# The range check's branch is moved from between the two layers to the end of the program, and layer 1's pools wait tile by tile

## The chip, the core and the metric

The kernel runs on one core of one Trainium2 chip. The metric is the device time of one execution in microseconds. Engines are named as in the profile: PE is TensorE's matmuls, PEld its weight loads, DVE is VectorE, ACT is ScalarE, POOL is GpSimd, SP is SyncE. A name with a q (SPq, PEldq, DVEq) is that engine's sequencer, which runs branches, waits, register loads and the issue of DMAs.

## What is computed

The input is x, float32 of shape (8, 256, 32, 32). Two layers follow each other:

```python
# layer 0, on images: attention and a gated convolutional block, each with a residual
a = attention(rms_norm(x))           # 1x1 conv -> 4 heads of softmax attention over 1024 positions, 3x3 depthwise conv
x = x + gamma1 * a
f = edffn(rms_norm(x))               # 1x1 conv -> 3x3 depthwise -> gelu(x1) * x2 -> 1x1 conv -> 8x8 FFT filter
x = x + gamma2 * f
# layer 1, on tokens t of shape (8, 1024, 256)
t = t + causal_attention(layer_norm(t))
t = t + mixture_of_8_experts(layer_norm(t))   # three 256x256 products each, gate from the mean over the batch
```

## The kernel before

The program is one straight line for each engine: all loops are unrolled when it is built. `pe`, `dve`, `act` and `pool` are wrappers (`InOrder`, recorded by the profile at L72) that keep their engine's instructions in the order in which the kernel calls them; what is called through `nc.` directly is placed by a scheduler. Loads and stores are issued by SP, in one queue.

**Layer 0.** The eight images are worked on in turn; attention of one image is woven with the convolutions of the one before. Softmax in layer 0 is taken without subtracting the maximum. That is exact as long as nothing overflows, so the sums and their reciprocals are kept in `accs`, and at the end of layer 0 they are compared with a limit. The last image's end runs alone: its last convolutions on DVE (`conv`, eight taps for each group), the products `pz`, `pf`, `py` on PE, and the additions into its tile `t` on DVE (from `py`). The image then goes to DRAM (`td`, L1114). A matrix `at`, needed by layer 1, is built from two weight matrices earlier in that stretch, in a tile `lin`, and also stored in DRAM (`at_d`, L1193).

**The branch.** `votes` (L1213, one matmul with one column) and `bad` (L1215, one element, on DVE) reduce the comparison to one integer. L1218 is

```python
with tc.If(nc.values_load(bad[0:1, 0:1]) > 0):
    layer0_shifted()
```

Each of the five engines loads `bad` into a register (TENSOR_LOAD), compares and branches (COMPARE_BRANCH). `layer0_shifted` is layer 0 again with the maximum subtracted. With the given inputs it is never run: all engines jump over it to a short block that brings the semaphores to the counts that the skipped part would have left and that waits for all DMAs of layer 0, the last store `td` among them.

**Layer 1.** Behind the branch the pool `wm` and the pools of layer 1 are opened. They stand on SBUF and PSUM that layer 0's pools had, and without `reuse_waits="tile"` their first instructions wait for what layer 0 left as a whole. SP issues, in this order, the vector `vec2` (L1231), `wrs`, `brs`, the first image `t` (L1376, 1 MB), `at` (L1380), `wv` (L1384), then two further images and the first expert weights `we` and `w`. `lower`, `mhalf1`, `sel` and `sel8` are constants that POOL builds.

The first image's layer norm is not woven with anything: PE transposes `t` into `tpt` (16 transposes), ACT copies to `zt`, DVE takes statistics (`st`, `mv`), POOL the power -1/2 (`y`, `r`), DVE scales `zt`, PE transposes back (`tpz`), ACT copies to `z`. Then PE forms keys (`pk`) and values (`pv`), and from there on the causal attention of one image is woven with the norms, keys and values of the next, and with `chores`, among them the splitting of the expert weights. At the head of DVE's share of layer 1 stand 19 small instructions that fold batch norm constants out of `vec2` (`bn_o` L175, `wrs`, `bn_s`, `s1a` to `s2b`, `bo`), and on ACT a table load and two square roots (L168).

**The expert stage.** Pools `hp`, `ps_a`, `ps_b`, `ps_q`, already with `reuse_waits="tile"`. PE is the bound; the last steps are an addition on DVE (`te`) and its store to `out` (L1808). The end of the program (L1986) is a block of waits for all semaphores and two barriers.

Of the kernel before, what the change touches and what calls it, by code (L numbers as in the profile page):

```python
# [104 lines left out]
def conv_attn_hybrid_kernel(  # L105
# [1111 lines left out]

    with tc.If(nc.values_load(bad[0:1, 0:1]) > 0):  # L1218
        layer0_shifted()

    z_d = [dram.tile([P, 2, 3, KC, HALF], F32, tag=f"zd{b}", name=f"zd{b}") for b in range(B)]
    u_d = [dram.tile([P, KC, N], F32, tag=f"ud{b}", name=f"ud{b}") for b in range(B)]
    wm = ctx.enter_context(tc.tile_pool(name="wm", bufs=1))
    more.append(wm.tile([P, NVEC - NVEC0], F32, name="vec2"))  # L1230
    nc.sync.dma_start(more[0], vecs[:, NVEC0:])  # L1231
    wrs = wm.tile([P, KC, NE], F32, name="wrs")
    nc.sync.dma_start(wrs, wr.rearrange("(k p) e -> p k e", p=P))
    brs = wm.tile([1, NE], F32, name="brs")
    nc.sync.dma_start(brs, br)
    wT = wm.tile([4 * NE, N], F32R, name="wT")
    feats = [wm.tile([P, KC, HALF], F32, name="feat0"), None]
    z2_last = wm.tile([P, KC, HALF], F32, name="z2_last")
    mhalf1 = wm.tile([P, NT], F32, name="mhalf1")
    nc.gpsimd.memset(mhalf1, -0.5)  # L1240

    NG, SLOTS = 2, NE // 2
    w_d = [[dram.tile([P, 3, KC, C], F32, tag=f"wd{e}_{l}", name=f"wd{e}_{l}") for l in range(3)] for e in range(NE)]
    w_in = {}

    def in_parts(e, l):

        return l != 1 or e % 2 == 1

    def load_expert(pool_, e, l):  # L1250

        tag = f"w{e % SLOTS}_{l}"
        if not in_parts(e, l):
            w_ = pool_.tile([P, KC, C], F32, tag=tag, name=tag, bufs=1)
            nc.sync.dma_start(w_, w2[e].rearrange("(k p) o -> p k o", p=P))
        else:
            w_ = pool_.tile([P, 3, KC, C], F32R, tag=tag, name=tag, bufs=1)
            nc.sync.dma_start(w_.bitcast(F32), w_d[e][l])
        w_in[e, l] = w_

    def stacked(dst, src, order):

        first = [order.index(i) for i in range(2)]
        dve.tensor_copy(dst[:, :, first[0]].bitcast(F32R), src)
        dve.tensor_sub(dst[:, :, first[1]].bitcast(F32R), src, dst[:, :, first[0]])
        for i, part in enumerate(order):
            if i not in first:
                dve.tensor_copy(dst[:, :, i], dst[:, :, first[part]])

    def upper(dst, src, eng=None, positive=False):  # L1270

        if eng is None:
            act.activation(dst[:, 0], src, AF.Relu if positive else AF.Copy, scale=DOWN)
        else:
            eng.tensor_scalar_mul(dst[:, 0], src, DOWN)

    def lower_part(dst, src, positive=False):
        high = dst[:, 0].bitcast(F32)
        if positive:
            dve.scalar_tensor_tensor(dst[:, 1], src, 0.0, high, ALU.max, ALU.subtract)  # L1280
        else:
            dve.tensor_sub(dst[:, 1], src, high)

    def difference(dst):
        dve.scalar_tensor_tensor(dst[:, 2], dst[:, 1].bitcast(F32), -STEP, dst[:, 0].bitcast(F32), ALU.mult, ALU.add)

    def layer_norm(src, dst, zt, room, bank):

        n = src.shape[2] // P
        mv = room([P, NT, 2], "mv", 2)  # L1290
        for i0 in range(0, n, 2):
            tp = bank([P, 2, C], "tpt")
            for i in range(2):
                for k in range(KC):
                    c0 = (i0 + i) * P
                    pe.transpose(tp[:, i, k * P : (k + 1) * P], src[:, k, c0 : c0 + P], ident)
            act.copy(zt[:, i0 : i0 + 2, :], tp)
            yield 0.6
            for i in range(i0, i0 + 2):
                st = room([P, 6], "st", 4)  # L1300
                dve.bn_stats(st, zt[:, i, :])
                dve.bn_aggr(mv[:, i, :], st)
            yield 0.6

        y = room([P, NT], "y1", 2)[:, :n]
        r = room([P, NT], "r1", 2)[:, :n]
        pool.tensor_scalar(y, mv[:, :n, 1], LN_EPS, None, ALU.add)
        pool.tensor_tensor(r, y, mhalf1[:, :n], ALU.pow)
        pool.tensor_mul(y, y, r)
        pool.tensor_mul(y, y, r)  # L1310
        pool.tensor_scalar(y, y, -0.5, 1.5, ALU.mult, ALU.add)
        pool.tensor_mul(r, r, y)

        for _ in range(4):
            yield 1.0

        def scaled(i0):
            for i in range(i0, i0 + 2):
                dve.tensor_scalar(zt[:, i, :], zt[:, i, :], mv[:, i, 0:1], r[:, i : i + 1], ALU.subtract, ALU.mult)

        scaled(0)
        yield 1.0
        scaled(2)
        yield 1.0
        for i0 in range(0, n, 2):
            if i0 + 4 < n:
                scaled(i0 + 4)
            tp = bank([P, KC, 2, P], "tpz")
            for i in range(2):
                for k in range(KC):  # L1330
                    pe.transpose(tp[:, k, i, :], zt[:, i0 + i, k * P : (k + 1) * P], ident)
            act.copy(dst[:, :, i0 * P : (i0 + 2) * P], tp.rearrange("p k i c -> p k (i c)"))
            yield 0.9

    def gate(h, room, bank):

        nt = NT // 2
        lg = bank([P, nt, NE], "lg")
        for i in range(nt):
            c0 = i * P  # L1340
            for k in range(KC):
                pe.matmul(lg[:, i, :], feats[h][:, k, c0 : c0 + P], wrs[:, k, :], start=(k == 0), stop=False)
            pe.matmul(lg[:, i, :], ones[0:1, :], brs, start=False, stop=True)
        yield 2.0
        ge = room([P, nt, NE], "ge", 1)
        gs = room([P, nt], "gs", 1)
        dve.tensor_reduce(gs, lg, AX.X, ALU.max)
        dve.tensor_sub(ge, lg, gs.unsqueeze(2).to_broadcast([P, nt, NE]))
        act.activation(ge, ge, AF.Exp)
        yield 1.0  # L1350
        dve.tensor_reduce(gs, ge, AX.X, ALU.add)
        dve.reciprocal(gs, gs)
        dve.tensor_mul(ge, ge, gs.unsqueeze(2).to_broadcast([P, nt, NE]))
        ge4 = room([P, nt, 4, NE], "ge4", 1)
        stacked(ge4, ge, (0, 1, 0, 1))
        yield 1.0
        pwT = bank([4 * NE, HALF], "pwT")
        for i in range(nt):
            pe.transpose(pwT[:, i * P : (i + 1) * P], ge4[:, i].rearrange("p a e -> p (a e)"), ident)
        dve.tensor_copy(wT[:, h * HALF : (h + 1) * HALF], pwT)  # L1360
        yield 0.5

    z = {}

    with ExitStack() as l1:
        wpool = l1.enter_context(tc.tile_pool(name="w1", bufs=1))
        one = l1.enter_context(tc.tile_pool(name="one1", bufs=1))
        two = l1.enter_context(tc.tile_pool(name="two1", bufs=2))
        tiny = l1.enter_context(tc.tile_pool(name="tiny1", bufs=4))
        ps_s = l1.enter_context(tc.tile_pool(name="ps_s1", bufs=2, space=PSUM))  # L1370
        ps_t = l1.enter_context(tc.tile_pool(name="ps_t1", bufs=2, space=PSUM))
        ps_m = l1.enter_context(tc.tile_pool(name="ps_m1", bufs=2, space=PSUM))

        def load_t(b):
            t[b] = two.tile([P, KC, N], F32, tag="t", name="t1", bufs=3)
            nc.sync.dma_start(t[b], t_d[b])  # L1376

        load_t(0)
        at = wpool.tile([P, KC, C], F32, name="at")
        nc.sync.dma_start(at, at_d)  # L1380

        def load_w(name, src):
            w_ = two.tile([P, KC, C], F32, tag=name, name=name, bufs=1)
            nc.sync.dma_start(w_, src.rearrange("(k p) o -> p k o", p=P))  # L1384
            return w_

        wv_s = load_w("wv", wvT)
        feats[1] = wpool.tile([P, KC, HALF], F32, name="feat1")
        load_t(1)


        lower = wpool.tile([P, P], F32, name="lower")
        nc.gpsimd.memset(lower, 1.0)
        nc.gpsimd.affine_select(
            out=lower, in_=lower, compare_op=ALU.is_ge, fill=0.0, base=0, pattern=[[-1, P]], channel_multiplier=1,
        )

        parts_w = two.tile([P, 3, KC, C], F32R, name="parts_w", bufs=1)
# [12 lines left out]
        def expert_parts():  # L1411

            for e in range(NE):
                for l, src in enumerate((w1, w2, wo)):
                    if not in_parts(e, l):
                        continue
# [75 lines left out]
        def until(what):  # L1492
            while what not in done:
                yield 0.7
# [152 lines left out]

# [336 lines left out]
```

## Time and profile before

| | us |
|---|---|
| median of 3 runs | 3183.1 (3177.89 to 3192.05) |
| the profiled execution: its own time | 3183.65 |
| its span, from the first to the last instruction | 3181.8 |
| PE busy | 2935.8 (92%) |
| DVE busy | 2390.2 (75%) |
| mean granted TensorE clock | 0.967 |

The profile is of one execution. Its time exceeds its span by 1.85 us. Times below are counted from the start of the span. A matmul's end is modelled, so busy time of PE says where PE has work, not how well it does it. A wait for several things is put down to the one that came last.

### The profile page before, as it was taken

What the parts mean: (1) busy time and instruction counts of PE and PEld (TensorE: products, weight loads), DVE (VectorE), ACT (ScalarE), POOL (GpSimd) and SP (SyncE); (2) the same over time, 40 slices, a digit from 0 to 9 for tenths busy, and PEclk for the clock granted to TensorE, in tenths of its full rate; (3) what the DMA queues carried; (4) which work ended last, traced back from release to release, by engine and by line L of the source; (5) the groups of instructions that cost most, each with busy time, mean ns of one, the idle gap of its engine ahead of it and who ended that gap; (6) DMA issues with size and microseconds to landing.
All of it is one profiled execution on the core that took longest, in us unless ns stands there. A gap on an engine that the chain in (4) does not pass through costs nothing.

```text
span 3181.8 us, 41598 instructions
## 1 busy us (share of the span) xinstructions
PE 2935.8 (92%) x16802; PEld 1938.8 (61%) x16802; DVE 2390.2 (75%) x3014; ACT 1565.1 (49%) x2312; POOL 341.0 (11%) x419
## 2 busy tenths in 40 slices
PE   5998899899898989868999999999999999999998
PEld 3654555555555555434666666677777777777776
DVE  1378877878787869664767665588988888888887
ACT  1554445555454536313333333365666666666665
POOL 1021211111111110001222222100000000000000
PEclk9998999999999999988999999999999999999999
DMA  5113030212112020002333221422112142211220
GB/s 152 55 27 80 27 80 27 72 36 62 46 47 61 28 66 8 17 14 101 125 131 132 106 103 54 176 76 78 69 67 82 64 172 86 99 67 66 93 73 27
DMA packets 63854, 234.85 MB, mean 74 GB/s; under 512 B 5590, under 2 KB 13862, under 8 KB 54822
## 3 DMA queue, kind: packets, MB, share of 16 engines
q1 hardware_dynamic: 63654, 232.12, 21.9%
q8 instruction: 134, 2.20, 0.3%
q14 instruction: 66, 0.54, 0.1%
HBM read 140.61 MB, written 91.49 MB: 73 GB/s over the span
## 4 chain that ended last, share of the span: by engine, by line
PE 49%; DVE 4%; ACT 1%; issue 0%; POOL 0%; SPq 0%; DMA 0%; ACTq 0%; DVEq 0%
PE pm L72 12%; PE pa L72 11%; PE q L72 11%; PE s L72 4%; PE po L72 4%; PE pv L72 2%; PE pk L72 2%; DVE zt L72 1%; DVE nm L72 1%; PE tp L72 1%; DVE pr L72 1%; PE tpz L72 1%; PE tpt L72 1%; DVE st L72 1%; ACT pr L72 1%
## 5 line engine op out<-in xcount | busy, mean ns | idle before, releaser
L72 PE MATMUL pa<-ze,w 128*128 128x512 f32 x1488 | 423.2, 393 | 0.0
L72 DVE SCALAR_TENSOR_TENSOR x<-hpad,vec,x 128x1024 f32<-128x1024 f32 x248 | 317.0, 1282 | 40.5 <-ACT x L72 33.5
L72 DVE SCALAR_TENSOR_TENSOR conv<-hpad,vec,conv 128x1024 f32<-128x1024 f32 x256 | 329.3, 1293 | 13.9 <-ACT conv L72 7.3
L72 PEld LDWEIGHTS pa<-ze,w 128*128 128x128 f32 x1488 | 278.2, 188 | 63.3 <-issue 3.1
L72 ACT ACTIVATE h<-pa,bn_o,s1a 128x512 f32<-128x512 f32 x256 | 198.7, 776 | 203.4 <-PE pa L72 203.4
L72 ACT ACTIVATE pT<-s 128x1024 f32<-128x1024 f32 x256 | 247.3, 1024 | 71.9 <-PE s L72 71.9
L72 PE MATMUL po<-pT,vT 128*32 128x256 f32 x4096 | 274.0, 385 | 0.0
L72 PE MATMUL q<-h2p,w 128*128 128x512 f32 x768 | 269.0, 459 | 0.0
L72 DVE SCALAR_TENSOR_TENSOR h<-pa,s1b,h 128x512 f32<-128x512 f32 x256 | 191.2, 747 | 93.9 <-PE pa L72 87.8
L72 PE MATMUL ph<-xn,piw 128*128 128x512 f32 x512 | 244.7, 615 | 3.1 <-DVE xn L72 1.6
L72 PE MATMUL pm<-h,w 128*128 128x512 f32 x512 | 240.8, 593 | 0.0
L72 PE MATMUL s<-kk,z 128*128 128x512 f32 x512 | 236.8, 594 | 4.1 <-DVE pr L72 4.1
L72 PE MATMUL q<-z_first,w 128*128 128x512 f32 x768 | 217.2, 391 | 2.7 <-DVE z_first L72 1.7
L72 PE MATMUL pm<-h1p,w 128*128 128x512 f32 x768 | 216.7, 390 | 0.5 <-DVE h1p L72 0.5
L72 DVE SCALAR_TENSOR_TENSOR o<-vpad,pe_w,o 128x1024 f32<-128x1024 f32 x128 | 163.5, 1282 | 45.5 <-ACT o L72 42.3
L72 PEld LDWEIGHTS q<-h2p,w 128*128 128x128 f32 x768 | 144.6, 188 | 83.1 <-issue 59.6
L72 PE MATMUL s<-qst,kst 128*128 128x256 f32 x1024 | 176.1, 314 | 14.5 <-DMA kst<-part 13.2
L72 ACT ACTIVATE hpad<-ph,pi_o 128x512 f32<-128x512 f32 x126 | 86.9, 689 | 182.9 <-PE ph L72 176.0
L72 PEld LDWEIGHTS po<-pT,vT 128*32 128x32 f32 x4096 | 120.8, 110 | 85.9 <-issue 4.2
L72 PEld LDWEIGHTS s<-qst,kst 128*128 128x128 f32 x1024 | 137.5, 193 | 47.8 <-issue 42.9
L72 PEld LDWEIGHTS q<-z_first,w 128*128 128x128 f32 x768 | 144.4, 188 | 34.4 <-DVE z_first L72 2.9
L72 PEld LDWEIGHTS pm<-h1p,w 128*128 128x128 f32 x768 | 144.7, 188 | 31.7 <-DVE h1p L72 0.9
(268 smaller groups left out, 5068.1 us busy)
## 6 DMA issues: line engine op xcount, KB each, us to landing
ze<-zd SPq DMA_DIRECT2D x29, 1536.0 KB, 6.4
qst<-part SPq DMA_DIRECT2D x32, 512.0 KB, 8.7
kst<-part SPq DMA_DIRECT2D x32, 512.0 KB, 14.9
te<-ud SPq DMA_DIRECT2D x32, 512.0 KB, 4.1
wd<-parts_w SPq DMA_DIRECT2D x20, 768.0 KB, 3.7
w<-wd SPq DMA_DIRECT2D x20, 768.0 KB, 4.6
zd<-parts SPq DMA_DIRECT2D x14, 1024.0 KB, 3.8
t<-in_x_dram SPq DMA_DIRECT2D x8, 1024.0 KB, 5.0
```

Of the source, the lines that this page charges most:

```text
L72: return self._tc.keep_in_program_order(method(*args, **kwargs))
```

## The change

Everything from the opening of `wm` to the end of the expert stage becomes a function `tokens(stack)`. It is called once without a condition, straight behind layer 0, and then a second time inside the branch, which now stands at the end of the program: if `bad` is set, layer 0 is run again with the maximum subtracted, and both later layers after it. `wm` and the seven pools of layer 1 get `reuse_waits="tile"`, so that a tile waits for the last users of the memory it stands on, and not for a whole pool. The first three loads of layer 1 (`t` of the first image, `at`, `wv`) are issued by POOL instead of SP, in POOL's program order. `wv` moves from one pool to another. What is left out (...) is the same code, indented once more.

```diff
-    with tc.If(nc.values_load(bad[0:1, 0:1]) > 0):
-        layer0_shifted()
+    NG, SLOTS = 2, NE // 2
     z_d = [dram.tile([P, 2, 3, KC, HALF], F32, tag=f"zd{b}", name=f"zd{b}") for b in range(B)]
     u_d = [dram.tile([P, KC, N], F32, tag=f"ud{b}", name=f"ud{b}") for b in range(B)]
-    wm = ctx.enter_context(tc.tile_pool(name="wm", bufs=1))
-    more.append(wm.tile([P, NVEC - NVEC0], F32, name="vec2"))
+    w_d = [[dram.tile([P, 3, KC, C], F32, tag=f"wd{e}_{l}", name=f"wd{e}_{l}") for l in range(3)] for e in range(NE)]
+
+    def tokens(stack):
+
+        wm = stack.enter_context(tc.tile_pool(name="wm", bufs=1, reuse_waits="tile"))
+        more[:] = [wm.tile([P, NVEC - NVEC0], F32, name="vec2")]
         nc.sync.dma_start(more[0], vecs[:, NVEC0:])
...
         with ExitStack() as l1:
-            wpool = l1.enter_context(tc.tile_pool(name="w1", bufs=1))
-            one = l1.enter_context(tc.tile_pool(name="one1", bufs=1))
-            two = l1.enter_context(tc.tile_pool(name="two1", bufs=2))
-            tiny = l1.enter_context(tc.tile_pool(name="tiny1", bufs=4))
-            ps_s = l1.enter_context(tc.tile_pool(name="ps_s1", bufs=2, space=PSUM))
-            ps_t = l1.enter_context(tc.tile_pool(name="ps_t1", bufs=2, space=PSUM))
-            ps_m = l1.enter_context(tc.tile_pool(name="ps_m1", bufs=2, space=PSUM))
+            wpool = l1.enter_context(tc.tile_pool(name="w1", bufs=1, reuse_waits="tile"))
+            one = l1.enter_context(tc.tile_pool(name="one1", bufs=1, reuse_waits="tile"))
+            two = l1.enter_context(tc.tile_pool(name="two1", bufs=2, reuse_waits="tile"))
+            tiny = l1.enter_context(tc.tile_pool(name="tiny1", bufs=4, reuse_waits="tile"))
+            ps_s = l1.enter_context(tc.tile_pool(name="ps_s1", bufs=2, space=PSUM, reuse_waits="tile"))
+            ps_t = l1.enter_context(tc.tile_pool(name="ps_t1", bufs=2, space=PSUM, reuse_waits="tile"))
+            ps_m = l1.enter_context(tc.tile_pool(name="ps_m1", bufs=2, space=PSUM, reuse_waits="tile"))
 
-            def load_t(b):
+            def load_t(b, queue=nc.sync):
                 t[b] = two.tile([P, KC, N], F32, tag="t", name="t1", bufs=3)
-                nc.sync.dma_start(t[b], t_d[b])
+                queue.dma_start(t[b], t_d[b])
 
-            load_t(0)
+            load_t(0, pool)
             at = wpool.tile([P, KC, C], F32, name="at")
-            nc.sync.dma_start(at, at_d)
-
-            def load_w(name, src):
-                w_ = two.tile([P, KC, C], F32, tag=name, name=name, bufs=1)
-                nc.sync.dma_start(w_, src.rearrange("(k p) o -> p k o", p=P))
-                return w_
-
-            wv_s = load_w("wv", wvT)
+            pool.dma_start(at, at_d)
+            wv_s = wpool.tile([P, KC, C], F32, name="wv")
+            pool.dma_start(wv_s, wvT.rearrange("(k p) o -> p k o", p=P))
             feats[1] = wpool.tile([P, KC, HALF], F32, name="feat1")
             load_t(1)
...
+    with ExitStack() as stack:
+        tokens(stack)
+
+    with tc.If(nc.values_load(bad[0:1, 0:1]) > 0):
+        layer0_shifted()
+        with ExitStack() as stack:
+            tokens(stack)
```

## The prediction

> **What bounds the kernel now.** I read the table of windows first, around the place of the branch and behind it. Its columns are the window, its length, busy time of each engine with its number of instructions, the granted TensorE clock, the DMA share and GB/s.
>
> ```profile
> 1353.00:1424.50 71.50, 47.70 (x148) 28.88 (x146) 54.01 (x55) 15.46 (x23) 0.00 (x0) 0.83 0.00 0
> 1424.50:1439.40 14.90, 0.00 (x0) 0.02 (x1) 3.02 (x20) 1.79 (x3) 4.62 (x7) 0.64 0.52 182
> 1439.40:1452.70 13.30, 6.55 (x33) 6.36 (x34) 6.73 (x24) 3.86 (x7) 2.73 (x6) 0.64 0.52 206
> 1452.70:1600.00 147.30, 142.84 (x568) 90.23 (x567) 92.01 (x219) 52.21 (x94) 23.89 (x36) 1.00 0.31 113
> 2100.00:3150.00 1050.00, 1049.20 (x4159) 778.18 (x4157) 904.16 (x974) 651.21 (x866) 5.23 (x6) 1.00 0.23 82
> ```
>
> PE is the bound from 1452.7 on: 142.84 of 147.3 us busy, and 1049.2 of 1050 in the expert stage. So whatever brings the keys' first matmul `pk` forward brings the end forward by as much. Between layer 0's last work and layer 1's first transpose PE does nothing for 14.9 us. The timeline of that stretch (start, duration, engine, line, what; in brackets the idle time before and its releaser) says why:
>
> ```profile
> 1422.71 1.77 DVE L72 SCALAR_TENSOR_TENSOR t<-py,vec,t 128x256 f32<-128x256 f32 x4 [0.64 <-PE py L72]
> 1424.51 0.32 SPq L1114 DMA_DIRECT2D td<-t  x1
> 1431.73 0.34 SPq L1231 DMA_DIRECT2D vec<-in_vecs_dram  x1
> 1433.69 2.25 POOL L1405 TENSOR_SCALAR_AFFINE_SELECT sel<-sel 32x1024 f32<-32x1024 f32 x2
> 1434.07 0.34 SPq L1376 DMA_DIRECT2D t<-td  x1
> 1435.00 1.05 DVE L175 TENSOR_TENSOR bn_o<-vec 128x16 f32<-128x16 f32 x2 [10.46 <-POOL sel L1405]
> 1439.41 3.29 PE L72 MATMUL tpt<-ident,t 128*128 128x128 f32 x16 [15.48 <-DMA at<-at_d]
> 1441.27 0.43 DVE L72 BATCH_NORM_STATS2 st<-zt 128x6 f32<-128x256 f32 x1 [2.84 <-ACT zt L72]
> 1452.67 3.60 PE L72 MATMUL pk<-z,at 128*128 128x512 f32 x8
> ```
>
> The last image is finished at 1424.48; the branch and its waits last to 1431.73; the load of `t`, fourth in SP's queue, goes out at 1434.07 and lands 5.3 us later. The instructions of the branch's own line price it (starts in us, durations in ns):
>
> ```profile
> L1218 SPq EVENT_SEMAPHORE  x8: 17/17/17, 1426.0 to 1430.1; - x8
> L1218 SPq TENSOR_LOAD <-bad x1: 522/522/522, 1424.9 to 1424.9; - x1
> L1218 ACTq COMPARE_BRANCH  x1: 50/50/50, 1425.1 to 1425.1; - x1
> L1218 PEldq COMPARE_BRANCH  x1: 5687/5687/5687, 1425.2 to 1425.2; - x1
> L1218 SPq COMPARE_BRANCH  x1: 50/50/50, 1425.5 to 1425.5; - x1
> L1218 ACTq EVENT_SEMAPHORE  x1: 17/17/17, 1431.4 to 1431.4; - x1
> ```
>
> After the comparison PE stands for 5.7 us and ACT for 6.3 (1425.1 to 1431.4); POOL and DVE do as ACT does. SP goes on after 0.5 us, since it has 47 instructions to jump over where the others have 569 to 4958. The trace's code fetches (queue q14) start at 1428.1, 3.0 us after the branches, when the packets of the 1 MB store `td` have just ended, and the engines go on 3 us after the fetch.
>
> **Part 1: layer 1's start.** In the built program PE, DVE and ACT have exactly the same instructions in the same order as on the path taken before; only SP's and POOL's queues differ, and the waits at this seam. PE's first `tpt` now waits for POOL's load of `t`, for the last `py` and for the last addition into `t` (its PSUM bank), and for nothing of the branch. POOL's load comes behind `mhalf1`, which waits for the last `ph` matmul (ends at 1392.5); everything else that it waits for, the store `at_d` included (issued at 1328.02), is older. So it is issued near 1392.6, on an engine with nothing to do there (0.00, x0 in the first window). The 1 MB loads of this stretch take 7.8 us (median) from SP: landing near 1400, 24 us early. `at` and `wv` follow with 37 us or more in hand. `vec2`, `wrs` and `brs` go out behind `at_d`. The first `tpt` can start 0.08 us after DVE's last addition, at 1424.56 instead of 1439.41: **-14.85 us**.
>
> What is late next: DVE's 19 small instructions, which the wait for the load hid, now stand between `bad` (ends 1424.54) and the first statistics. They took 3.43 us (1435.00 to 1438.43). 0.80 of it was one `bn_o` of 0.97 beside a twin of 0.16, while POOL's `sel` select ran; 0.41 was a wait for ACT's square roots, whose data now lie ready 90 us before. Left are 2.2 us, to 1426.75; the statistics want to start 1.86 us behind `tpt` (1439.41 to 1441.27), at 1426.42. Difference: **+0.35 us**. ACT's table load (1.28 us) fits behind its last `zf` at 1418.9.
>
> POOL's constants move too. `lower` runs in layer 0, `sel` (a memset of 0.94, two selects of 1.09 each) behind the loads near 1393, beside DVE's taps, which are the path there; the cast of 1.03 waits for `pz` (1415.5) and meets little. The tap `conv` takes 1.285 us, up to 1.516 beside POOL's copies; the `bn_o` row lost 0.80 to a select. Bound: 0 to 2.2 us. I take **+1.0**, between the tap's row and `bn_o`'s.
>
> SP's queue behind the last `td` is now two weight loads, then `t` of the second and third image, issued by about 1427. Landing took 7.8 to 10.9 us there; the second image's transposes come 29 us behind the first's, near 1453. Nothing waits. `kk` now waits for `td` to land (5.3 us, 1429.8) but is not due before 1439.
>
> The clock is granted at 0.64 in both middle windows, and at 1.00 just when `pk` starts. Full clock in the layer norm would save at most half of `tpz`'s 3.40 us; a half clock lasting 6.8 us longer would cost the keys and values 3.4. Bound -1.6 to +3.4, taken **0**.
>
> **Part 2: the branch at the end.** The last store is issued from 3178.05 to 3178.42; before, SP then waited for it to land (3180.9), and the barriers ended at 3181.8. Now SP loads `bad` (0.52) and branches (0.05) at 3179.0, and it has 402 instructions to jump over, so it stands like the others. At 6.3 us: 3185.3; eight waits at 0.066, 0.5; the end's twelve, 0.7; barriers as before, 0.8; end at 3187.4, **+5.6**. The store's landing is hidden in it. The lower bound: if half of the 6.3 was queueing behind `td`'s 1 MB (the store here is half as large), the stall is near 3.4 and the end comes at +2.7. I take **+4.5**, since a store is in flight here too. PE and ACT reach their branches 2 us or more earlier and are not last; DVE's comes 0.4 us before SP's.
>
> [...] The row of POOL's first window is idle, so nothing in it delays a load. [...] For the branch the row is 5.7 to 6.3 us. [...]
>
> **The sum.** -14.85 + 0.35 + 1.0 + 0 + 4.5 = -9.0 us; with all bounds favourable -13.4 (0 for POOL, -1.6, +2.7), with all unfavourable -3.3 (2.2, 3.4, 5.6). The profiled execution's 3183.65 becomes 3174.65, and the median, 0.55 lower, **3174**. That is 0.28%, under the 0.5% (15.9 us) that a measurement of this kernel can tell from no change.
>
> **Rivals.** *The end costs nothing.* The engines stall 0.5 us as SP did, and the clock recovers: -14.85 + 0.35 - 1.6 + 0.6 = -15.5, so 3167.6, on the edge of what can be told. For it: SP's 0.5 us row. Against: PE's 5.69, and 402 instructions against 47. Chance 0.20.
>
> *POOL's load is late* (the one that ends slower). No row shows a DMA issued by POOL. Each us by which `t` lands after 1424.5 costs one us; it turns into a loss at 1433.5, 41 us after its issue. If it needs six times SP's 7.8 us (47), it lands at 1439.4 and all of part 1 is lost: +4.5 and more, 3188; slower by 0.5% only above 58 us. For it: the untried queue. Against: 32 us of an idle queue and idle DMA (share 0.00 there). Chance 0.10.
>
> *The change moves no load*, because the reused memory is in use until layer 0's end: excluded by the built program's waits, except through a wait that I misjudge: no gain, +4.5, 3188; in the same 0.10.
>
> **Numbers.** My forecast has 0.70 and lies between 3169.7 and 3179.8; three runs of before spread from -5 to +9 us around their median, which widens it on both sides. 3164 to 3185 takes in the first rival with some of that spread and leaves out most of the late load. Faster by over 0.5% (below 3167.2): the first rival lies 0.4 us from that line, and with the spread I count two thirds of it, 0.13, and 0.07 for a tail of mine: 0.20. Slower (above 3199): the late load beyond 58 us, 0.07. Within: 0.73.
>
> **What would show it.** Right: PE's idle time before the first `tpt` below 1 us; POOL's load issued near 1393; `pk` near 1439; the windows behind as long as before; a stall of 3 to 6 us after SP's comparison at the end, and the span 8 to 10 us shorter. Wrong: `tpt` waiting for POOL's load, taps `conv` well over 1.5 us, keys and values at half clock, or an end that goes on within 1 us.

## The result and the profile after

The changed kernel takes 3175.33 us (median of 7 runs, 3171.40 to 3176.36), the kernel before beside it 3183.73 (7 runs). The ratio is 0.9974, with a 95% interval of 0.9964 to 0.9983: faster by 5.4 to 11.5 us, and under the 0.5% that was counted as a difference that can be told from one comparison. Two further sets of the same two kernels gave 0.9971 each time.

The profiled execution of the changed kernel took 3171.40 us, its span 3169.4 (3181.8 before), at a mean clock of 0.969. First the table of windows, cut as before around the seam:

```profile
1352.70:1423.80 71.10, 46.97 (x145) 28.55 (x144) 54.58 (x55) 17.25 (x26) 7.09 (x8) 0.83 0.06 22
1423.80:1437.30 13.50, 5.22 (x32) 5.04 (x33) 8.63 (x45) 3.68 (x7) 2.74 (x6) 0.75 0.75 272
1437.30:1584.60 147.30, 142.84 (x568) 90.23 (x567) 92.02 (x219) 52.17 (x93) 23.88 (x36) 1.00 0.31 113
2084.60:3134.60 1050.00, 1049.20 (x4160) 778.16 (x4159) 904.28 (x974) 650.74 (x866) 5.24 (x6) 1.00 0.23 82
```

The two windows of 14.9 and 13.3 us have become one of 13.5, in which PE has 5.22 us of work. In the stages behind, PE has the same busy time to 0.01 us. The first window, where POOL had nothing, now holds 7.09 us of POOL. Next the timeline of that stretch:

```profile
1391.76 0.81 POOL L72 DMA_DIRECT2D t<-td  x1 [0.65 <-issue]
1393.84 0.97 POOL L1392 MEMSET sel<- 32x1024 f32 x1
1394.71 2.21 DVE L72 TENSOR_TENSOR hid<-x,conv 128x512 f32<-128x512 f32 x2
1394.88 2.98 POOL L1394 TENSOR_SCALAR_AFFINE_SELECT sel<-sel 32x1024 f32<-32x1024 f32 x2
1396.84 11.35 DVE L72 SCALAR_TENSOR_TENSOR conv<-hpad,vec,conv 128x1024 f32<-128x1024 f32 x8
1422.04 1.77 DVE L72 SCALAR_TENSOR_TENSOR t<-py,vec,t 128x256 f32<-128x256 f32 x4 [0.64 <-PE py L72]
1423.84 0.33 SPq L1114 DMA_DIRECT2D td<-t  x1
1423.91 1.94 PE L72 MATMUL tpt<-ident,t 128*128 128x128 f32 x16 [0.66 <-PE votes L1213]
1425.73 0.42 DVE L72 BATCH_NORM_STATS2 st<-zt 128x6 f32<-128x256 f32 x1
1437.34 7.03 PE L72 MATMUL pk<-z,at 128*128 128x512 f32 x16
3162.84 0.37 SPq L1784 DMA_DIRECT2D out_dram<-te  x1
```

POOL's load of `t` goes out at 1391.76. The last addition ends at 1423.81 and `tpt` starts 0.10 us later. Its wait is now put down to `votes`, PE's own matmul, and no longer to a DMA. Beside POOL's two selects DVE's groups `hid` and `conv` take 2.21 and 11.35 us, where the same groups took 1.29 and 10.52 in the profile before:

```profile
1396.24 1.29 DVE L72 TENSOR_TENSOR hid<-x,conv 128x512 f32<-128x512 f32 x2
1397.45 10.52 DVE L72 SCALAR_TENSOR_TENSOR conv<-hpad,vec,conv 128x1024 f32<-128x1024 f32 x8
```

Then the end of the changed kernel, in the rows of the branch's line (starts in us, durations in ns):

```profile
L1856 SPq EVENT_SEMAPHORE  x8: 17/17/17, 3167.0 to 3167.5; - x8
L1856 PEldq COMPARE_BRANCH  x1: 3875/3875/3875, 3160.0 to 3160.0; - x1
L1856 ACTq COMPARE_BRANCH  x1: 50/50/50, 3160.3 to 3160.3; - x1
L1856 ACTq EVENT_SEMAPHORE  x1: 17/17/17, 3163.1 to 3163.1; - x1
L1856 SPq COMPARE_BRANCH  x1: 50/50/50, 3163.8 to 3163.8; - x1
```

PE stands for 3.9 us, ACT for 2.8 (3160.3 to 3163.1), SP for 3.1 (3163.9 to 3167.0). From the last store's issue to the end it takes 6.6 us; before, it was 3.75.

The two profiles put instruction beside instruction give the span's 12.4 us as a sum. Ahead of 192 us, where nothing differs: -1.35. From there to the last addition: +0.68. From the last addition to `tpt` (14.93, now 0.10): -14.83. From `tpt` to `pk` (13.26, now 13.43): +0.17. From `pk` to the last store (1725.4, now 1725.5): +0.11. Behind that (3.75, now 6.61): +2.86.

### The profile page after: what moved, and what is told of

Read it like the earlier page. It is cut to its first block, busy times and chain, and to the rows that moved or that the text cites. A ratio compares the mean times of both kernels' runs of the same rounds, so it can differ in the third digit from the quotient of the medians.

```text
span 3169.4 us, 41581 instructions
## 1 busy us (share of the span) xinstructions
PE 2933.1 (93%) x16802; PEld 1936.7 (61%) x16802; DVE 2390.7 (75%) x3014; ACT 1564.5 (49%) x2312; POOL 343.9 (11%) x422
## 4 chain that ended last, share of the span: by engine, by line
PE 77%; DVE 14%; ACT 3%; POOL 2%; DMA 2%; issue 2%; SPq 0%; ACTq 0%; DVEq 0%; POOLq 0%
PE pm L72 12%; PE pa L72 11%; PE q L72 11%; PE po L72 10%; PE s L72 8%; PE ph L72 6%; DVE conv L72 3%; PE pq L72 3%; PE sums L72 3%; DVE o L72 2%; PE pz L72 2%; PE pv L72 2%; PE pk L72 2%; DVE x L72 1%; DVE zt L72 1%
## 5 line engine op out<-in xcount | busy, mean ns | idle before, releaser
L72 PEld LDWEIGHTS pa<-ze,w 128*128 128x128 f32 x1488 | 278.2, 188 | 63.3 <-issue 3.1
```

The lines of the kernel that those rows point to most:

```text
L72: return self._tc.keep_in_program_order(method(*args, **kwargs))
```

## The experiments

Three sets were run, each on one chip and beside the kernel before. Ratios are to the kernel before of the same set. The four pieces of the last columns are from one profile each: A from the first tap `conv` of the last image's end to the last addition, B from there to `pk`, C from `pk` to the issue of the last store, D from there to the end.

| | median us | ratio (95%) | A | B | C | D |
|---|---|---|---|---|---|---|
| before | | 1 | 62.4 | 28.2 | 1725.4 | 3.75 |
| changed, first profile | 3175.33 | 0.9974 (0.9964 to 0.9983) | 63.3 | 13.5 | 1725.5 | 6.6 |
| set 1: before 3181.69 | | | | | | |
| changed again | 3171.82 | 0.9971 (0.9961 to 0.9981) | 63.3 | 13.5 | 1725.5 | 6.6 |
| no branch | 3168.96 | 0.9964 (0.9952 to 0.9976) | 63.3 | 13.5 | 1725.5 | 4.0 |
| short branch, in the middle | 3178.73 | 0.9992 (0.9983 to 1.0001) | 61.4 | 23.2 | 1729.4 | 4.0 |
| loads from SP | 3181.93 | 1.0003 (0.9994 to 1.0012) | 63.1 | 22.0 | 1727.4 | 7.2 |
| set 2: before 3184.70 | | | | | | |
| `sel` later | 3176.07 | 0.9971 (0.9961 to 0.9981) | 61.4 | 13.5 | 1728.8 | 6.9 |
| pools wait as a whole | 3189.22 | 1.0019 (1.0007 to 1.0030) | 61.4 | 29.2 | 1726.9 | 7.5 |
| before, with pools and POOL loads | 3184.54 | 0.9997 (0.9988 to 1.0007) | 61.4 | 29.2 | 1730.1 | 4.2 |
| short branch, at the end | 3170.09 | 0.9952 (0.9934 to 0.9970) | 63.6 | 13.6 | 1729.3 | 4.0 |
| set 3: before 3181.49 | | | | | | |
| changed a third time | 3172.59 | 0.9971 (0.9958 to 0.9983) | 63.6 | 13.6 | 1729.3 | 6.6 |
| last store by ACT | 3172.98 | 0.9972 (0.9961 to 0.9984) | 63.8 | 13.7 | 1726.3 | 5.6 |
| both: `sel` later, store by ACT | 3173.96 | 0.9974 (0.9962 to 0.9985) | 62.4 | 13.6 | 1729.7 | 6.0 |

### What the branch costs at the end

The changed kernel unaltered:

> The changed kernel once more, as the base of this set. Theory (boundary -14.7, POOL's two selects beside DVE's taps +0.7, end +2.8): about -11 us against the kernel before, ratio 0.9965, and in the profile again two DVE instructions stretched by 0.8 to 0.9 us beside the selects, the first transpose within 0.2 us of the last image addition, and all engines standing 2.7 to 3.9 us after the comparison at the end. The 1.35 us by which the first profile was ahead already at 192 us would be chance and come out different here. Rival (that lead belongs to the change, as its program is twice as long): 1.3 to 1.4 us again.

It came near the theory, at -9.9 us where about -11 was expected. Its profile was ahead of before's by 2.9 us at the first tap, where the first one was ahead by 1.5. The kernels with other edits, none of which touches what comes before, stood there from 5.6 us ahead to 4.8 behind. So the lead doesn't belong to the change: at 192 us the kernel without a branch, whose program is no longer than before's, and the kernel before with the two other parts of the change were each ahead by 1.3 us as well. Half clock is part of such differences (116 to 137 us of it lay ahead of 1353 us in these profiles), but not of the first pair's: both have 23.9 us of it ahead of 192 us, and 0.9 of their 1.35 us has arisen by 50 us. What that comes from stays open.

The branch taken out:

```diff
-    with tc.If(nc.values_load(bad[0:1, 0:1]) > 0):
-        layer0_shifted()
-        with ExitStack() as stack:
-            tokens(stack)
```

> The changed kernel without the branch and the copy of the program behind it (the repetition for images out of range is left out). Theory: the end falls back to what it was before, 3.75 us from the issue of the last store to the last instruction instead of 6.56, so -2.8 us against the changed kernel, and nothing else moves. Rival (the branch is hidden behind the landing of the last store, and the longer end has to do with the eight waits and the barriers of a longer program): -0.5 us or less. Second rival (a program twice as long costs something all along, in code fetches): more than -4 us.

The median fell by 2.9 us (3171.82 to 3168.96) and D by 2.6, with A, B and C as they were. The intervals of the two ratios overlap, so it is the profile's D that carries this. The end of 2.9 us is the branch, and a program twice as long costs nothing beside it that shows.

The branch kept, but over one small store:

```diff
     with tc.If(nc.values_load(bad[0:1, 0:1]) > 0):
-        layer0_shifted()
-        with ExitStack() as stack:
-            tokens(stack)
+        nc.sync.dma_start(ov[B - 1][:, 0, :P], ident)
```

> The changed kernel with a branch over one small store at its end, in place of the copy of the program (the repetition for images out of range is left out). Theory (a far jump's code fetch is what costs): no stall over 0.3 us behind the comparisons; the end is bound by the landing of the last store again, and the kernel is 2.0 to 2.8 us faster than the changed one. Rival (the flag's load and the comparison cost whatever the distance): the stall of about 3 us stays, within 0.5 us of the changed kernel.

The rows of its branch show what is gone:

```profile
L1856 PEldq COMPARE_BRANCH  x1: 223/223/223, 3161.5 to 3161.5; - x1
L1856 SPq COMPARE_BRANCH  x1: 50/50/50, 3165.3 to 3165.3; - x1
L1856 SPq EVENT_SEMAPHORE  x1: 17/17/17, 3165.5 to 3165.5; - x1
```

PE's comparison takes 0.22 us and not 3.9, SP goes on after 0.2 us and not 3.1. The flag's load stays (0.5 us). D is that of the kernel without a branch (4.0 us). The traces have code fetches (queue q14) at the end where the kernel jumps over the copy of the program: 7 from 3155 us on in the changed kernel, 8 from 3160 on in the next experiment, but one from 3165 on in the kernel before, with no branch there, and none at the end of this one. **The stall comes with the far jump and its fetches, and is gone without them**; that the engine stands for the fetch is my reading of the two together. The ratio, 0.9952, is better than these 2.6 us explain (0.9971 less 0.0008 is 0.9963, which its interval holds).

The changed kernel with more data in flight at the end:

```diff
                                 nc.sync.dma_start(to, t)
+                                if (G, h, b) == visits[-1]:
+                                    for d in (0, 1):
+                                        nc.sync.dma_start(z_d[d][:, h, 0], t)
```

> The changed kernel with the last 512 KB tile stored twice more (to scratch memory that is not read again) right behind its last store, so that 1.5 MB and not 0.5 MB are in flight when SP jumps at the end. Theory (the code fetch queues behind the data, which is why the old branch stood 5.7 to 6.3 us behind a 1 MB store and this one 2.8 to 3.9): SP's stall behind its comparison grows from 3.1 us to 5 or more; PE and ACT, which jump before the stores, stay at 2.8 to 3.9. Rival (the stall is the same wherever the jump is, and the old one was longer for another reason): 3.1 us again. The end comes later in both, by the landing of the two stores.

D is 10.3 us in the one execution that was taken of it. SP's stall became 3.7 us, and its load of the flag 1.10 in place of 0.49:

```profile
L1859 SPq EVENT_SEMAPHORE  x8: 17/17/17, 3169.8 to 3170.3; - x8
L1859 SPq COMPARE_BRANCH  x1: 50/50/50, 3166.0 to 3166.0; - x1
```

The expected 5 was not reached, because SP came to its comparison only 2 us ahead of the end of the data. The starts of the code fetches show the two parts of the stall (the trace doesn't name a fetch's engine; it is taken from the time). At the changed kernel's end SP's fetch starts 1.5 us behind the comparison (ACT's, with no data in flight, 1.2, and 0.9 in the kernel's two other profiles), and the engine goes on 1.6 us behind that start (ACT 1.6 to 1.8). With the added stores it starts 2.1 us behind, as the data end, and the engine again goes on 1.6 us later. In the middle of the kernel before it started 3.0 us behind, as `td` ended, and the engines went on 3.2 us after the start. So the first part of what the old branch cost more, 3.0 against 1.5, goes with the data: in both cases the fetch started as they ended. The second part, 3.2 against 1.6, came where four fetches started within 0.1 us; that this is the reason wasn't tried.

### Which part of the change carries the gain

The loads from SP's queue instead of POOL's:

```diff
-            load_t(0, pool)
+            load_t(0)
             at = wpool.tile([P, KC, C], F32, name="at")
-            pool.dma_start(at, at_d)
+            nc.sync.dma_start(at, at_d)
             wv_s = wpool.tile([P, KC, C], F32, name="wv")
-            pool.dma_start(wv_s, wvT.rearrange("(k p) o -> p k o", p=P))
+            nc.sync.dma_start(wv_s, wvT.rearrange("(k p) o -> p k o", p=P))
```

> The changed kernel with the first loads of t, at and wv in SP's queue in place of POOL's; everything else stays, and t then stands behind the last store of layer 0 in that queue. Theory (the early load is what the boundary's gain rests on, and POOL's queue is what makes it early): t goes out near 1424.9, lands 5.3 to 6 us later, the first transpose comes near 1430.5 instead of 1423.9, and the clock falls to half in the wait: +6.5 us against the changed kernel, up to +8. Rival (the branch alone was the loss, and SP's queue would have served as well): within 1 us of the changed kernel.

It was +10.1 us against the changed kernel of the set, and the whole gain was gone (1.0003).

```profile
1423.74 2.53 SPq L1370 DMA_DIRECT2D t<-td  x3
1431.30 3.65 PE L72 MATMUL tpt<-ident,t 128*128 128x128 f32 x16 [9.07 <-DMA t<-td]
```

The load goes out 1 us behind the last addition, as expected, but takes 7.5 us and not 5.3 to 6, beside the 1 MB of `td` ahead of it and the next two images behind it. (In the kernel before it also had two images behind it, but `td` had landed, and it took 5.2.) B grew by 8.4 us. Of the rest of the profile's difference, 2.0 us is in C, whose lengths are taken up below, and 0.6 in D.

The pools' waits taken back:

```diff
-        wm = stack.enter_context(tc.tile_pool(name="wm", bufs=1, reuse_waits="tile"))
+        wm = stack.enter_context(tc.tile_pool(name="wm", bufs=1))
...
-            two = l1.enter_context(tc.tile_pool(name="two1", bufs=2, reuse_waits="tile"))
+            two = l1.enter_context(tc.tile_pool(name="two1", bufs=2))
```

(and so for the other six pools of layer 1)

> The changed kernel with layer 1's pools waiting for layer 0's pools as a whole (reuse_waits taken out of wm and the layer 1 pools): the branch alone moved, the loads still in POOL's queue. Every engine has the same instructions in the same order. Theory: POOL's first constant then waits for the last store of layer 0 to land (1429.1), the load of t goes out near 1430 and lands near 1435.8, and the first transpose starts there: +11 to +12 us against the changed kernel, so about the time of the kernel before, 0 to +3 us. Rival (the branch was the loss): within 2 us of the changed kernel.

```profile
1418.42 0.10 POOL L1236 MEMSET mhalf<- 128x8 f32 x1 [13.77 <-DVE t L72]
1424.90 0.81 POOL L72 DMA_DIRECT2D t<-td  x1 [6.38 <-DVE bo L72]
1435.01 3.65 PE L72 MATMUL tpt<-ident,t 128*128 128x128 f32 x16 [16.30 <-DMA t<-td]
```

It is slower than the kernel before, by 0.19% (0.07 to 0.30). At +4.5 us it lies outside the 0 to +3 that were expected. POOL's constants now wait for DVE's `t`, and its load of `t` for the landing of `td` (1424.29) and the small DVE instruction `bo` behind that: it goes out at 1424.90, 5.6 us behind the last addition (1419.28 in this profile), as the theory had it. The load then needs 10.1 us, beside SP's two images that go out at 1424.78. I had expected 5.8 us for it.

The other two parts without the branch's move, on the kernel before:

```diff
-            nc.sync.dma_start(t[b], t_d[b])
+            queue.dma_start(t[b], t_d[b])
-        load_t(0)
+        load_t(0, pool)
```

(`at` and `wv` likewise, and `reuse_waits="tile"` in `wm` and the seven pools)

> The kernel before, its branch where it was, with the two other parts of the change: per-tile waits in layer 1's pools and the first loads of t, at and wv in POOL's queue. Theory (no load can pass the branch): POOL goes on at 1431.4, its load of t goes out near 1432.3 instead of 1434.1, and the first transpose comes 1 to 2 us earlier than before: -1 to -2 us against the kernel before. Rival (per-tile waits do most of it): -8 us or more.

No difference (0.9997, 0.9988 to 1.0007); the expected 1 to 2 us didn't come.

```profile
1432.12 0.81 POOL L72 DMA_DIRECT2D t<-td  x1 [0.81 <-issue]
1439.74 1.51 PE L72 MATMUL tpt<-ident,t 128*128 128x128 f32 x6 [16.31 <-DMA t<-td]
```

POOL's load went out 8.1 us behind the last addition in place of SP's 9.6, but landed 7.5 us later in place of 5.2, beside SP's loads of the next images at 1432.7. The earlier issue in a second queue was paid back in a slower landing.

A short branch in the middle came of a second kernel, whose branch over one instruction the scheduler puts where `bad` is ready:

```diff
     with tc.If(nc.values_load(bad[0:1, 0:1]) > 0):
-        layer0_shifted()
-        with ExitStack() as stack:
-            tokens(stack)
+        nc.vector.memset(bad, 0)
```

> The changed kernel with a branch over one instruction in place of the copy of the program (the repetition for images out of range is left out); the program puts it between layer 0 and layer 1, where the old branch stood. Theory (what costs is the code fetch behind a jump to a far place): no engine stands longer than 0.3 us after its comparison; each still pays the load of the flag (0.5) and the comparison (0.05 to 0.08), so the first transpose comes 0.7 to 0.9 us after the last image addition instead of 0.1, the end is 3.75 us again, and the sum is -2.0 us against the changed kernel. Rival (what costs is the comparison or the emptying of an engine's queue, wherever it jumps): engines stand 3 to 6 us in the middle, and the kernel is 0 to 4 us slower than the changed one.

No engine stood: PE's comparison took 0.24 us. The sum was still wrong by 9 us: +6.9 against the changed kernel, and not -2.0.

```profile
1421.00 0.81 POOL L72 DMA_DIRECT2D t<-td  x1 [30.87 <-DVE s2b L72]
1429.14 3.65 PE L72 MATMUL tpt<-ident,t 128*128 128x128 f32 x16 [10.30 <-DMA t<-td]
```

POOL's load has to stand behind the branch, since POOL takes it too. It goes out 1.6 us behind the last addition (1419.39) and lands 8.0 us later. I had left out that the branch, which all five engines take, is a wall here for every queue, even when PE's comparison takes 0.24 us. **The loss of the old place is mostly that no load could pass it**: with the same pools and POOL's loads, B is 29.2 us with the stall (the kernel of the paragraph before), 23.2 without it, and 13.5 with the load ahead of everything.

So any two of the three parts gave nothing or a loss. Here the load must stand in a queue that isn't behind `td` (B is 22.0 us where it does), its tile must not wait for layer 0 as a whole (29.2), and the branch must not stand ahead of it (29.2, or 23.2 with the short one).

### POOL's constants beside the taps

```diff
-            sel = two.tile([4 * NE, NE, P], F32, tag="pT", name="sel")
-            nc.gpsimd.memset(sel, 0.0)
...
             def expert_parts():
 
+                sel = two.tile([4 * NE, NE, P], F32, tag="pT", name="sel")
+                pool.memset(sel, 0.0)
...
```

> The changed kernel with POOL's constants sel (memset, two selects, cast) written behind the second image's layer norm, where PE is the bound, in place of beside DVE's last taps. Theory: the two DVE instructions that took 1.60 and 2.10 us take 0.69 and 1.28 again, the taps end 1.7 us earlier, and the last image addition, after what the clock takes or gives, 0.7 to 1.7 us earlier: about -1 us against the changed kernel. Rival (the taps had slack behind them): 0. Second rival (the selects now hold up DVE work of the attention): slower by up to 1.7 us.

```profile
1393.71 1.29 DVE L72 TENSOR_TENSOR hid<-x,conv 128x512 f32<-128x512 f32 x2
1394.92 10.53 DVE L72 SCALAR_TENSOR_TENSOR conv<-hpad,vec,conv 128x1024 f32<-128x1024 f32 x8
```

Both groups are back at their old durations, and A is 61.4 us against 63.3: the selects cost 1.9 us here. The ratio is the same as the changed kernel's, and in this profile C is 3.3 us longer. Whether that belongs to the edit was asked with a third profile of the changed kernel:

> The changed kernel a third time, as the base of this set. From the keys' first matmul to the issue of the last store four profiles (before, and the changed kernel's) take 1725.4 to 1725.5 us, and six others 1726.9 to 1730.1, all of which show the half clock return in the attention 116 to 119 us after the keys began, and not first after 191. Theory (this is chance, or belongs to the chip that a set runs on): this profile shows either the one or the other, and the ratio to the kernel before stays 0.997. Rival (the length of that stretch belongs to the kernel): 1725.5 again.

The same kernel now has C at 1729.3 us. The two rows are the window from 116.4 to 123.2 us behind `pk`, in the first profile of the changed kernel and in this one:

```profile
1553.74:1560.54 6.80, 6.11 (x31) 4.62 (x32) 4.68 (x7) 4.70 (x7) 1.79 (x2) 1.00 0.05 19
1552.82:1559.62 6.80, 6.25 (x18) 4.95 (x19) 3.77 (x5) 3.03 (x4) 1.98 (x2) 0.50 0.00 0
```

The clock is 1.00 in the one and 0.50 in the other. From there on the half clock returns about every 75 us in the attention, for 3.4 or 6.8 us: 116, 191, 267, 345 us behind `pk` in this profile, and first at 191 in the other. So C moves by 3.8 us between two profiles of one kernel, and by 4.7 over all. Four profiles had the long first stretch (before, the changed kernel twice, and the one without a branch), ten the short one. The rival that ties C to the kernel falls, and with it the reading that `sel` gives its gain back. Whether the execution or the chip decides is not settled: on the chip of set 1 both stretches came, in different kernels, and on those of sets 2 and 3 the short one alone. The medians don't show the gain either; 1.9 us lies inside their intervals.

### A version from both findings

```diff
-                                nc.sync.dma_start(to, t)
+                                (act if (G, h, b) == visits[-1] else nc.sync).dma_start(to, t)
```

> The changed kernel with the very last store issued by ACT in place of SP; nothing else moves. Theory (SP's turn behind its store is what the end waits for: it reads the flag and jumps only behind the store's issue, then stands 3.1 us, then does eight waits one after the other): SP now jumps some 10 us before the end, ACT stands 2.8 us behind the store, and the end comes 4.7 to 5.0 us after the last store's issue in place of 6.6: -1.7 us. Rival (the end is bound by DVE's jump or by the landing): -0.5 us or less.

> Both edits: POOL's constants sel behind the second image's layer norm, and the last store from ACT. Theory: -1.9 us in layer 0 (as the profile with the constants moved showed) and -1.7 at the end, -3.6 us against the changed kernel where the attention costs both the same. Rival (the gain in layer 0 is given back in the attention, by a half clock that comes sooner or by the selects beside DVE there): -1.7 us, with 2 us more between the keys' first matmul and the last store.

SP now jumps some 26 us ahead of the end, and D falls to 5.6 and 6.0 us, not to 4.7 to 5.0: ACT stands 3.2 and 3.5 us behind its own flag and comparison, where 2.8 was expected, and the last store lands only 3.4 us after its issue. In the medians neither can be told from the changed kernel (0.9972 and 0.9974 against 0.9971). The kernels with lower ratios, without a branch or with a short one at the end, leave the repetition out, so they are no versions to keep. No version that computes everything beat the changed kernel.

## Why the prediction was right, step by step

**The start of layer 1: -14.85 predicted, -14.83 in the profiles.** POOL's load went out within 1 us of the predicted time and landed in 5.3 us, 27 us ahead of its use. `tpt` starts 0.10 us behind the last addition (0.08 was expected). The experiments bear out what it rested on: with the load from SP or behind the pools' waits the gain is gone.

**DVE's small instructions: +0.35 predicted, +0.17 from `tpt` to `pk`.** They end at 1425.7 and the first statistics follow at once, 0.6 us after ACT's first copy is ready. So they are the last wait there, as predicted. But the transposes ran at a granted clock of 1.00, where it had been 0.58 (1.94 us in place of 3.29), and gave that back: from `tpt` to the first statistics it took 1.82 us, where it had been 1.86. The +0.17 arose behind the statistics.

**POOL's constants: +1.0 predicted, 1.7 on the taps.** This term was too small. One `hid` took 1.60 us in place of 0.69, one `conv` 2.10 in place of 1.28, one for each select. (In the third profile the selects met two `conv`, of 2.01 and 1.99 us, which makes 1.4.) The `bn_o` row had the price (0.80 for one select), and two selects at that price would have been 1.6; I took a value between it and a row of copies. The pair of profiles shows only +0.86 in A, since the half clock lay longer on the last `pz` in before (6.74 us at a granted 0.55, now 5.85 at 0.63); of the profiles without the constants at that place four stand at 61.4 and two, before among them, at 62.4, and all with them at 63.1 to 63.8.

**The clock: 0 predicted.** Around the seam it was (`tpz` 3.49 us in place of 3.40, keys and values at 1.00 in both). Over the whole program it makes profiles differ, by up to 4.7 us in the attention alone. The -1.35 us ahead of 192 us are not the clock's, since both profiles have the same time at half clock there. The bound I gave, -1.6 to +3.4, was for the keys and values alone and too small for a run.

**The end: +4.5 predicted, +2.9 measured, 2.6 to 2.9 by taking the branch out.** The stall came, 3.1 us behind SP's comparison, and the size was off by 1.6 us. My lower bound (+2.7, a stall near 3.4) had the reason right: the old stall held a wait for the 1 MB store, with the fetches starting 3.0 us behind the comparisons as its packets ended. I went above it because a store is in flight here too; with that store the fetch started 0.3 to 0.6 us later only (1.5 us behind the comparison, where ACT's without it started at 0.9 to 1.2).

**The sum.** -9.0 us predicted. The profiles say -12.4, of which -1.35 lies ahead of the change; the medians of the three comparisons say -8.4, -9.9 and -8.9. The structural terms, with the taps at 1.9, add up to -14.83 + 0.17 + 1.9 + 2.9 = -9.9. The two errors, +0.9 on the taps and -1.6 at the end, went against each other, so the total was better than its terms, and that is luck.

**The rivals.** *The end costs nothing* fell by the kernel without a branch. *POOL's load is late* fell by the first timeline line. *The change moves no load* is what the pools waiting as a whole do: at 4.5 us over the kernel before it came at the rival's price, as a change with one part missing. There the load did go out 4 us sooner behind the last addition than in the kernel before, and lost it in its landing.

**POOL beside DVE, and the branches.** From POOL's idle row I took it that nothing would delay its loads. Here the three issues took 0.81, 0.55 and 0.74 us beside the taps, and the load landed in 5.3 us: no delay shows. What POOL's constants did to DVE differs from one to the next: the memset of `sel` (0.97 us) left the `conv` beside it at 1.285, each select held one DVE instruction up (1.60 us in place of 0.69, 2.10 in place of 1.28), and the first `hid`, which had begun before the first select, took 0.69 while that select took 1.49 in place of 1.09. Why these differ was not tried.

For the branch I went by the row of 5.7 to 6.3 us. In the profiles the far jumps held an engine for 2.5 to 6.3 us, the short branches for 0.05 to 0.24.

## What to carry to other kernels

Here a branch that is never taken cost most by what couldn't pass it (of the 15.7 us that lie between a B of 29.2 and one of 13.5, 9.7 were left without the stall): look for the loads that stand behind it in any queue, and count the stall only then. Edits that each free one of several waits in a row can be worth nothing until the last is made (here two of three were), so try them together before dropping any. When a change is worth 0.3%, line up two profiles instruction by instruction and take out what two profiles of one kernel differ by before crediting a term.

## What the hardware showed that was not expected

- The far jumps' stalls had two parts, up to the start of the code fetch (0.9 to 1.2 us behind ACT's comparison with idle DMA engines, 3.0 behind a 1 MB store) and 1.6 to 1.8 us from there (3.2 where four fetches started within 0.1 us).
- In the attention, with PE busy for 94 to 97% of the time, half clock came back about every 75 us for 3.4 or 6.8 us, and whether it began 116 or 191 us behind `pk` differed between profiles of one kernel, taken in different sets.
- A 1 MB load took 5.3 us with no other transfer of that size beside it, and 7.5 to 10.1 us beside two others of that size in a second queue or behind a store of that size.
